# FFN grid values turned in bfloat16 apart from their scales, the first pass rebuilt, and a new order of work

## The chip, the core and the metric

The kernel runs on one core of a Trainium2 chip. A core has a matrix engine (TensorE, PE in the profile, with its weight loads shown as PEld), a vector engine (VectorE, DVE), a scalar engine (ScalarE, ACT), a general engine (GpSimd, POOL) and an engine that starts transfers (SyncE, SP; its queue is SPq). Each works through its own instructions in the order in which they were written into its queue, and waits on semaphores for the others. The metric is the device time of one execution in microseconds (us); the kernel before takes 1528.81 us, the median of three runs (1525.49 to 1529.01).

## What is computed

A small transformer stack on x of 4 x 2048 x 256 in float32:

```python
x = x + attn_a(layernorm(x))      # random-feature form; q and k divided by the norm of the whole tensor
x = x + ffn(layernorm(x))
x = x + attn_b(layernorm(x))      # 16 heads, attention over the first axis of 4
x = x + ffn(layernorm(x))

def fp4_quant_dequant(x):         # blocks of 16 along the last axis
    scale = max(max(abs(xb)) / 6, 1e-12)
    idx = searchsorted(MID, abs(xb / scale))
    return GRID[idx] * sign(xb) * scale     # GRID = 0, .5, 1, 1.5, 2, 3, 4, 6

def ffn(x):                       # 256 -> 704 -> 256
    gate = q(x) @ q(w_gate).T
    y = q(x) @ q(w_up).T
    return q(silu(gate) * y) @ q(w_down).T  # q is fp4_quant_dequant
```

In attn_a the quotient of the two feature maps needs, besides x, only the two norms of q and k over all tokens. They are found from the gram matrix of the normalized x, before any token can be projected.

## The kernel before

The 2048 positions are cut into 16 groups (`NJ`) of 128; a group holds the 4 tokens (`S`) of each of its positions, 128 partitions by 4 x 256. `first_pass` goes over all groups once: it loads x (tile `x`, L312), takes mean and variance on DVE (`bn_stats` L595, `bn_aggr` L596 into `moments`), the inverse root on POOL (`roots`, L363 and around), normalizes on ACT (L392) and adds up the gram in two PSUM banks on PE (L563). Beside this the weights are loaded, folded (L818), centred (L850) and, for the FFN, quantized and turned (L709 to L762). At its end the gram is weighed with the weights (L916 to L919), multiplied and summed on DVE (`sum_products`, L939 and L940), the norms' roots are taken on ACT, and the weights of the feature maps are joined by them (`join_weights`, L986 and L987). Only then can the first projection (L1076, `wvz`) start.

`group(j)` writes the work of one group: `attention_a`, an FFN, `attention_b`, a second FFN. An FFN has `ffn_in`, once for the group's four tokens, and `ffn_tile`, once for each token. Both call `quantize` (from L1108). For the hidden values (128 x 704) it runs:

- DVE: block maxima (L398) and their reciprocals (L399) into `sh`; ACT: maxima by 1/6 (L1123)
- DVE: values over scales (L403, into `qa`, float32)
- ACT: steps of the grid (L409, into `qm`, bfloat16)
- DVE: two passes (L416 `to_sum`, L419 `from_sum`) that leave the grid value, signed, in `qa`
- POOL: grid values by scales (L1151, in place in `qa`)
- PE: six transposes of 128 x 128 in float32 into two PSUM banks (L1349); ACT: two copies into `hqT` (L1361)
- PE: six matmuls of the down projection (L1372)

The input (128 x 1024, tiles `xn`, `qax`, `qmx`, `sx`) goes the same way and is turned by `turn` (L1053, L1060) into a tile of the pool `turned`, from which the gate and up projections read (L1294). A float32 matmul appears as two records in the trace, a transpose as one.

The order is made when the program is built. Each piece of work is an `op` with an engine, an estimated duration, a rank and what it reads and writes. `Plan.order` simulates the engines and takes, for each engine that is free, the ready op of lowest rank whose buffers are to be had; DVE and POOL ops with `port=True` are not laid beside each other. A group's ranks begin at the six numbers of its row in the table `BEGIN` (attention a, first FFN's input and tiles, attention b, second FFN's input and tiles). `order(24)` tries 24 orders, one by the ranks and 23 with ranks shaken by random numbers, and keeps the one that ends first in this simulation. The chosen order is the order of instructions on every engine. The pools have few tiles (two `qax`, one `qmx`, four `qa`, two `qm`, five `sh`, two `hqT`, eight PSUM banks), and an op that needs one waits until the last user of it has ended.

Of the kernel before, what the change touches and what calls it, by code (L numbers as in the profile page):

```python
# [57 lines left out]
class Plan:  # L58
# [55 lines left out]
    def order(self, tries):  # L114

        ends = [(self.order_of(i)[0], i) for i in range(tries)]
        return self.order_of(min(ends)[1])[1]

    def order_of(self, seed):
# [57 lines left out]
        while left:  # L177
# [56 lines left out]
            if not times:  # L234
                return math.inf, []
# [14 lines left out]
        return now, [i for _, i in out]  # L250
# [3 lines left out]
def kernel(  # L254
# [74 lines left out]

    moments = one([P, NJ, S, 2], "moments")  # L330
    half_moments = one([P, 6], "half_moments")
# [25 lines left out]
    def root_of(v, y, t, half):  # L357

        power(v, y, half)
        newton(v, y, t)  # L360

    def power(v, y, half):
        nc.gpsimd.tensor_tensor(y, v, half, ALU.pow)  # L363

    def newton(v, y, t):
        nc.gpsimd.tensor_mul(t, y, y)
        nc.gpsimd.tensor_mul(t, t, v)
        nc.gpsimd.tensor_scalar(t, t, -0.5, 1.5, ALU.mult, ALU.add)
        nc.gpsimd.tensor_mul(y, y, t)
# [48 lines left out]
    def from_sum(a, m):  # L418
        nc.vector.scalar_tensor_tensor(a, m, FLOOR, a, ALU.max, ALU.subtract)  # L419
# [16 lines left out]
    tiles("qax", 2, [P, S * D], fp)  # L436
    tiles("qmx", 1, [P, S * D], fp, BF16)
    tiles("sx", 3, [P, 3, S * D // BLK], fp)
    tiles("sil", 2, [P, HF], fp)
    tiles("qa", 4, [P, FF], fp)  # L440
    tiles("qm", 2, [P, FF], fp, BF16)
    tiles("sh", 5, [P, 3, FB], fp)
    tiles("hqT", 2, [P, 6, P], fp)
# [14 lines left out]
    def first_pass():  # L458
# [5 lines left out]
        for b in XN:  # L464
            nc.gpsimd.memset(b.ap[:, :, D : D + 1], 1.0)
        WQK, PROD, WNAT = (plan.given("pp", 0) for _ in range(3))
# [16 lines left out]
        sums, part, ssq, bsq, rn = (  # L483
            one([P, 2], t) for t in ("sums", "part", "ssq", "bsq", "rn")
        )
# [55 lines left out]
        def normalized_products(n, j):  # L541
# [15 lines left out]
            def products(n=n, xn=xn):  # L557
                for s in range(S):
# [11 lines left out]
            op(  # L570
                "PE",
                2.62,
                AHEAD + 3.0 * n + 9,
                products,
                [(xn, s) for s in range(S)],
                [(b, 0) for b in GRAM],
            )

        for n, j in enumerate(order):
            X = kept[j % len(xs_of)]  # L580
            xj = X.ap
            own = [(X, s) for s in range(S)]
            op(
                "SP",
                1.8,
                AHEAD + 3.0 * n - 40.0,
                lambda xj=xj, j=j: load_x(xj, j),
                (),
                own,
                land=3.0,  # L590
            )

            def stats(xj=xj, j=j):
                for s in range(S):
                    nc.vector.bn_stats(half_moments, xj[:, s, :])  # L595
                    nc.vector.bn_aggr(moments[:, j, s, :], half_moments)  # L596

            op("DVE", 2.35, AHEAD + 3.0 * n, stats, own, [("moments", j)])

            if n == 0 or n % 2:  # L600
                js = slice(j - 1 if n > 1 else j, j + 1)

                def roots(js=js):
                    mean, var = (moments[:, js, :, i] for i in range(2))
                    y, off, v, t = (norm_tiles["a"][:, js, i, :] for i in range(2, 6))
                    nc.gpsimd.tensor_scalar(v, var, 1.0, LN_EPS, ALU.mult, ALU.add)
                    root_of(v, y, t, nhalf[:, : js.stop - js.start, :])
                    nc.gpsimd.tensor_mul(off, mean, y)
                    nc.gpsimd.tensor_scalar(off, off, -1.0, 0.0, ALU.mult, ALU.add)

                js = range(js.start, js.stop)
                op(
                    "POOL",
                    3.3,
                    AHEAD + 3.0 * n + 3,
                    roots,
                    [("moments", i) for i in js],
                    [(("a", i), "rstd") for i in js],
                )
                for i in js:  # L620
                    normalized_products(order.index(i), i)
# [265 lines left out]
        def sum_biases():  # L887
            v = squares.ap[:, : 2 * D]
            nc.vector.tensor_mul(v, grow, grow)
            nc.vector.tensor_reduce(  # L890
                bsq, v.rearrange("p (t m) -> p t m", t=2), AX.X, ALU.add
            )

        op(
            "DVE", 1.4, AHEAD + 30.0, sum_biases, [(GROW, 0)], [(squares, 0), ("bsq", 0)], port=True
        )
        def take_g00():
            nc.vector.tensor_copy(g00, gram[0][:, :P])
# [5 lines left out]
        def take_sums():  # L904
            nc.vector.tensor_scalar_mul(sums[:, 0:1], gram[0][:, D : D + 1], 2.0)
            nc.vector.tensor_scalar_mul(sums[:, 1:2], gram[1][:, P : P + 1], 2.0)
# [4 lines left out]
        for c in range(KC):  # L911
            mm = plan.buf("mm")

            def weigh(c=c, mm=mm):
                if c == 0:
                    nc.tensor.matmul(mm.ap, g00, wqkA[:, 0, :], start=True, stop=True)  # L916
                else:
# [13 lines left out]
                    ALU.mult,  # L931
                    ALU.add,
                ),
                [(mm, 0), (GROW, 0), (G, 2)],
                [(PROD, c)],
            )

# [767 lines left out]
```

## Time and profile before

| | |
|---|---|
| median of three runs | 1528.81 us |
| the profiled execution's own time | 1528.71 us |
| its span, first to last instruction | 1526.9 us |
| mean granted clock of TensorE | 0.995 |

The page is one execution on the chip. Busy time is summed by engine and by groups of like instructions; a group's row has the line, the engine and the operation, what it writes and reads, partitions by elements, how often, busy time and mean duration, and then the engine's idle time just before them with what ended it. The two groups of this kernel's rows that fill the most time are the gate and up projections (L1294, 637.6 us) and the down projection (L1372, 350.1 us), both on PE; DVE has no such row, but five of about 120 to 130 us each, most of them passes of the quantization. Ends of matmuls are modelled and include the drain of the pipeline, so the time for which a matmul holds PE is read from start to start.

A row of stretches has the stretch, its length, then for PE, PEld, DVE, ACT and POOL the busy time and number of instructions, then the granted clock (1.00 is full), the busy share of the DMA engines and GB/s.

### The profile page before, as it was taken

The page shows a single profiled execution, that of the slowest core. Times are in us where ns is not written, and L with a number is a line of the kernel's source. Part 1 is how long each engine was busy: PE and PEld are TensorE (multiplying, and loading weights), DVE is VectorE, ACT ScalarE, POOL GpSimd, SP SyncE. Part 2 cuts the span into 40 slices and gives each one's busy share as a digit, 9 for nine tenths or more (in the row PEclk, how much of TensorE's full clock was granted, in tenths as well). Part 3 has the DMA queues.
Part 4 walks back from the last instruction along what each step waited for, and adds up shares of the span by engine and source line. Part 5 has one row for each costly group of instructions (what it writes and reads, how often), then busy time and mean ns, then how long its engine had stood idle before and what let it go on. Part 6 is the DMA issues. An engine that isn't in the chain of part 4 may idle for free.

```text
span 1526.9 us, 18822 instructions
## 1 busy us (share of the span) xinstructions
PE 1500.2 (98%) x6354; PEld 1074.1 (70%) x6354; DVE 1402.8 (92%) x2288; ACT 812.5 (53%) x1742; POOL 699.2 (46%) x738
## 2 busy tenths in 40 slices
PE   6989999999999999999999999999999999999999
PEld 5846766777676677777767776776766677777776
DVE  7988999999999999999998999989898999999995
ACT  5655655465463564464645445564646563554452
POOL 5333443346544552635446264453534435454531
PEclk9999999999999999999999999999999999999999
DMA  8300000000000000000000010000000000000000
GB/s 251 105 10 1 1 1 0 8 4 22 4 22 4 4 8 8 21 1 21 22 7 8 7 36 4 8 7 25 8 4 4 1 4 4 6 10 4 21 18 21
DMA packets 28976, 27.68 MB, mean 18 GB/s; under 512 B 3536, under 2 KB 28624, under 8 KB 28880
## 3 DMA queue, kind: packets, MB, share of 16 engines
q1 hardware_dynamic: 28880, 26.49, 5.5%
q8 instruction: 50, 0.82, 0.2%
q14 instruction: 46, 0.38, 0.1%
HBM read 18.09 MB, written 8.39 MB: 17 GB/s over the span
## 4 chain that ended last, share of the span: by engine, by line
PE 83%; DVE 12%; ACT 2%; issue 2%; DMA 1%; POOL 1%; SPq 0%; ACTq 0%; DVEq 0%; POOLq 0%
PE bank L1294 35%; PE bank L1076 20%; PE bank L1372 19%; PE bank L1349 5%; PE bank L1053 4%; DVE half_moments L595 1%; DVE qa L416 1%; DVE qa L403 1%; DVE h L1326 1%; DVE pp L1477 1%; DVE sh L398 1%; DVE qa L419 1%; DVE sc L1484 0%; DVE moments L596 0%; DVE pp L1603 0%
## 5 line engine op out<-in xcount | busy, mean ns | idle before, releaser
L1294 PE MATMUL bank<-wguT,turned 128*128 128x352 f32 x2048 | 637.6, 459 | 0.6 <-DVE h L1326 0.6
L1294 PEld LDWEIGHTS bank<-wguT,turned 128*128 128x128 f32 x2048 | 381.4, 190 | 193.8 <-issue 11.3
L1151 POOL TENSOR_TENSOR qa<-qa,sh 128x704 f32<-128x704 f32 x128 | 211.9, 1656 | 408.8 <-DVE qa L419 333.7
L1372 PE MATMUL bank<-wdT,hqT 128*128 128x256 f32 x1536 | 350.1, 379 | 0.0
L1372 PEld LDWEIGHTS bank<-wdT,hqT 128*128 128x128 f32 x1536 | 289.5, 190 | 51.9 <-issue 4.3
L1315 ACT ACTIVATE sil<-bank 128x352 f32<-128x352 f32 x256 | 117.0, 459 | 127.5 <-PE bank L1294 113.2
L409 ACT ACTIVATE qm<-qa 128x704 bf16<-128x704 f32 (+2 forms) x136 | 106.2, 783 | 104.1 <-DVE qa L403 102.0
L1361 ACT COPY hqT<-bank 128x256 f32<-128x256 f32 (+1 forms) x256 | 110.9, 481 | 85.2 <-PE bank L1349 84.4
L1326 DVE TENSOR_TENSOR h<-sil,bank 128x352 f32<-128x352 f32 x256 | 128.6, 510 | 27.1 <-PE bank L1294 16.8
L1585 POOL TENSOR_TENSOR pp<-vg,sc 128x1024 f32<-128x1024 f32 x64 | 132.4, 2088 | 19.1 <-DVE tok L1606 17.8
L416 DVE SCALAR_TENSOR_TENSOR qa<-qm,qa 128x704 f32<-128x704 bf16 (+2 forms) x136 | 130.6, 961 | 7.8 <-ACT qm L409 7.2
L403 DVE SCALAR_TENSOR_TENSOR qa<-sh,h 128x704 f32<-128x704 f32 x128 | 128.6, 1008 | 2.0
L419 DVE SCALAR_TENSOR_TENSOR qa<-qm,qa 128x704 f32<-128x704 bf16 (+2 forms) x136 | 124.1, 914 | 2.1
L1076 PE MATMUL bank<-wvz,turned 128*128 128x512 f32 x256 | 121.0, 608 | 3.6 <-DVE wvz L987 2.4
L398 DVE TENSOR_REDUCE sh<-h 128x44 f32<-128x748 f32 x128 | 119.0, 930 | 3.6
L1060 ACT COPY turned<-bank 128x512 f32<-128x512 f32 x160 | 87.0, 592 | 63.4 <-PE bank L1053 58.0
L1076 PE MATMUL bank<-wqkB,turned 128*128 128x512 f32 x256 | 120.4, 593 | 0.0
L1151 POOL TENSOR_TENSOR qax<-qax,sx 128x1024 f32<-128x1024 f32 x32 | 68.2, 2133 | 101.9 <-DVE qax L419 96.6
L1349 PEld LDWEIGHTS bank<-ident,qa 128*128 128x128 f32 x768 | 90.7, 141 | 29.3 <-issue 13.1
L1349 PE MATMUL bank<-ident,qa 128*128 128x128 f32 x768 | 105.7, 273 | 0.5 <-ACT turned L1060 0.3
L348 ACT ACTIVATE dev<-x,norms_f 128x256 f32<-128x256 f32 x128 | 65.0, 508 | 44.5 <-DVE x L342 41.5
L1076 PEld LDWEIGHTS bank<-wvz,turned 128*128 128x128 f32 x256 | 48.0, 195 | 50.6 <-issue 39.9
(168 smaller groups left out, 2119.6 us busy)
## 6 DMA issues: line engine op xcount, KB each, us to landing
x<-in_L_attn_a_x_dram SPq DMA_DIRECT2D x24, 512.0 KB, 4.3
out_dram<-x SPq DMA_DIRECT2D x64, 128.0 KB, 1.7
hqT<-in_L_ffn_w_down_dram SPq DMA_DIRECT2D x2, 352.0 KB, 2.8
hqT<-in_L_ffn_w_gate_dram SPq DMA_DIRECT2D x5, 128.0 KB, 4.5
hqT<-in_L_ffn_w_up_dram SPq DMA_DIRECT2D x5, 128.0 KB, 2.1
pp<-in_L_attn_a_Wq_dram SPq DMA_DIRECT2D x2, 256.0 KB, 4.2
pp<-in_L_attn_a_Wk_dram SPq DMA_DIRECT2D x2, 256.0 KB, 5.1
wvz<-in_L_attn_a_Wv_dram SPq DMA_DIRECT2D x1, 256.0 KB, 5.1
```

Source lines behind the costliest of these rows:

```text
L398: nc.vector.tensor_reduce(amax, src, AX.X, ALU.max, apply_absolute_value=True)
L403: nc.vector.scalar_tensor_tensor(blocks(a), over_blocks(rs), -6.0 * BELOW, src, ALU.mult, ALU.mult)
L416: nc.vector.scalar_tensor_tensor(a, m, FLOOR, a, ALU.max, ALU.add)
L419: nc.vector.scalar_tensor_tensor(a, m, FLOOR, a, ALU.max, ALU.subtract)
L1076: nc.tensor.matmul(bank.ap[:, :n], lhs.ap[:, c, s * P : (s + 1) * P], w[:, c, :], start=(c == 0), stop=(c == KC - 1),)
L1151: lambda: nc.gpsimd.tensor_mul(blocks(a.ap), blocks(a.ap), over_blocks(q.ap[:, 1, :])),
L1294: nc.tensor.matmul(bank.ap[:, :HF], xqT.ap[:, c, s * P : (s + 1) * P], w[:, c, cols], start=(c == 0), stop=(c == KC - 1),)
L1315: lambda g=g, sil=sil: nc.scalar.activation(sil.ap, g.ap[:, :HF], AF.Silu),
L1326: lambda u=u, sil=sil, half=half: nc.vector.tensor_mul(h.ap[:, half * FB // 2 : (half + 1) * FB // 2, :BLK], blocks(sil.ap), blocks(u.ap[: ...
L1349: nc.tensor.transpose(bank.ap[:, (i - i0) * P : (i - i0 + 1) * P], qa.ap[:, HC[i] : HC[i] + P], ident,)
L1372: nc.tensor.matmul(o.ap[:, :D], hqT.ap[:, i, :], wdT[:, i, :], start=(i == 0), stop=(i == 5),)
L1585: nc.gpsimd.tensor_mul(pv.ap.rearrange("p t (n e) -> p t n e", e=HD), vg.ap[:, :, :D].rearrange("p t (n e) -> p t n e", e=HD), over_blocks ...
```

## The change

Four things.

**The FFN's values are turned without their scales.** `from_sum` now writes the grid values, which are exact in bfloat16, into the bfloat16 tile. The scale product before the transposes goes, and with it the ACT product by 1/6. The grid values are turned by bfloat16 transposes (into one bank read as bfloat16), and ACT copies them back to the bfloat16 tile (`qm`, `qmx`). The maxima are turned by themselves (`scales_turned`: one float32 transpose, a copy by 1/6 on ACT into `sT`), and SP spreads each turned row over the 16 partitions of its block by DMA, straight into `hqT` or `turned`: eight rows of 128 numbers, each written 16 times, 64 KB in one transfer; six transfers for a hidden tile, eight for an input. POOL then multiplies the copied values into the spread scales, in place, and PE's projection reads the product.

**The first pass.** The first load of x comes in four pieces. `bn_aggr` goes: `bn_stats` writes its two halves' means and variances for all groups into an unused part of a tile, and mean and variance are put together for a group at once, for the first three groups on DVE with the root on ACT, for the later ones in pairs on POOL. The gram's products are an op for each token instead of one for all four. The bias terms of the norms are summed ahead (`times_biases`), and each half of the weighed gram is multiplied and summed in one instruction with `accum_out`; five small matmuls add up the parts. The weights are joined in two halves.

**The pools** are cut differently.

**The order.** `order(0)` takes the one order by the ranks, and `BEGIN` has other numbers; the first group's ranks now lie among those of the first pass (which run from -350 up).

```diff
-    order = plan.order(24)
+    order = plan.order(0)
...
-    tiles("qax", 2, [P, S * D], fp)
-    tiles("qmx", 1, [P, S * D], fp, BF16)
-    tiles("sx", 3, [P, 3, S * D // BLK], fp)
+    tiles("qax", 1, [P, S * D], fp)
+    tiles("qmx", 2, [P, S * D], fp, BF16)
+    tiles("sT", 2, [S * D // BLK, P], fp)
+    tiles("sx", 2, [P, 3, S * D // BLK], fp)
...
-    tiles("qa", 4, [P, FF], fp)
-    tiles("qm", 2, [P, FF], fp, BF16)
-    tiles("sh", 5, [P, 3, FB], fp)
-    tiles("hqT", 2, [P, 6, P], fp)
+    tiles("qa", 3, [P, FF], fp)
+    tiles("qm", 4, [P, 6 * P], fp, BF16)
+    tiles("sh", 4, [P, 3, FB], fp)
+    tiles("hqT", 3, [P, 6, P], fp)
...
-        (160, 226, 202, 285, 260, 357),
-        (242, 270, 276, 370, 420, 434),
...
+        (-192, -130, -62, -192, 24, 94),
+        (30, 12, 85, 183, 69, 266),
...
-            op(
-                "POOL",
-                us["scale"],
-                at + 6,
-                lambda: nc.gpsimd.tensor_mul(
-                    blocks(a.ap), blocks(a.ap), over_blocks(q.ap[:, 1, :])
-                ),
...
+                "DVE",
+                us["pass"],
+                at + 4.1,
+                lambda: from_sum(a.ap, *2 * (m.ap[:, : n],)),
                 [(a, 0)],
+                [(m, 0)],
                 port=True,
+            )
...
+        def scales_turned(at, q, n, dst, pieces):
+            bank, sT = plan.buf("bank"), plan.buf("sT")
...
+                lambda: nc.tensor.transpose(bank.ap[:n, :P], q.ap[:, 0, :], ident),
...
+                lambda: nc.scalar.mul(sT.ap[:n], bank.ap[:n, :P], 1.0 / 6.0),
...
+            def spread():
+                for to, g in pieces:
+                    nc.sync.dma_start(
+                        to(),
+                        sT.ap[g : g + P // BLK].unsqueeze(1).to_broadcast([P // BLK, BLK, P]),
+                    )
+            op(
+                "SP",
+                0.45 * len(pieces),
+                at + 1,
+                spread,
+                [(sT, 0)],
+                [(dst, "scale")],
+                land=2.0,
+            )
...
+            def turn_hidden():
+                for i, f in enumerate(HC):
+                    nc.tensor.transpose(
+                        bank.ap.bitcast(BF16)[:, i * P : (i + 1) * P],
+                        qm.ap[:, f : f + P],
+                        ident16,
+                    )
...
+                lambda: nc.scalar.copy(
+                    qm.ap, bank.ap.bitcast(BF16)[:, : 6 * P]
+                ),
...
+                lambda: nc.gpsimd.tensor_mul(
+                    hqT.ap, hqT.ap, qm.ap.rearrange("p (c n) -> p c n", n=P)
+                ),
+                [(qm, 0), (hqT, "scale")],
+                [(hqT, 0)],
+                port=True,
```

And of the first pass:

```diff
-            def stats(xj=xj, j=j):
                 for s in range(S):
-                    nc.vector.bn_stats(half_moments, xj[:, s, :])
-                    nc.vector.bn_aggr(moments[:, j, s, :], half_moments)
...
+                for s0, s1 in [(s, s + 1) for s in range(S)] if n == 0 else [(0, S)]:
...
+                        lambda xj=xj, j=j, s=s: nc.vector.bn_stats(
+                            moments[:, j, s, :], xj[:, s, :]
+                        ),
...
+            if n >= SOON:
+                op("POOL", 4.4, at + 3.0, lambda cut=cut: roots_later(cut), seen, done)
+            else:
...
+                op("DVE", 0.8, at + 0.5, lambda cut=cut: variances(cut), seen, done)
...
+                    lambda y=y, v=v: nc.scalar.activation(y, v, AF.Sqrt),
...
+                op("DVE", 1.0, at - 30.0, lambda cut=cut: inverses(cut), (), done)
...
-            nc.vector.tensor_mul(prod, prod, wqkA)
-            nc.vector.tensor_reduce(
-                part, prod.rearrange("p c (t m) -> p t c m", t=2), AX.XY, ALU.add
-            )
...
+                    nc.vector.scalar_tensor_tensor(
+                        prod[:, c, cols],
+                        mm.ap[:, cols],
+                        1.0,
+                        wqkA[:, c, cols],
+                        ALU.mult,
+                        ALU.mult,
+                        accum_out=part[:, 3 + c, t : t + 1],
+                    )
```

## The prediction

> **What bounds the kernel now.** I read the page's busy shares first, then its chain.
>
> ```profile
> PE 1500.2 (98%) x6354; PEld 1074.1 (70%) x6354; DVE 1402.8 (92%) x2288; ACT 812.5 (53%) x1742; POOL 699.2 (46%) x738
> ...
> PE 83%; DVE 12%; ACT 2%; issue 2%; DMA 1%; POOL 1%; SPq 0%; ACTq 0%; DVEq 0%; POOLq 0%
> ```
>
> TensorE (PE) is nearly always busy and carries 83% of the chain, but VectorE (DVE) at 92% is close behind. An average hides stages, so next the busy time by stretch (columns: PE, PEld, DVE, ACT, POOL, clock, DMA share, GB/s).
>
> ```profile
> 0.00:20.00 20.00, 6.89 (x32) 6.00 (x32) 14.00 (x47) 5.87 (x10) 9.14 (x40) 1.00 0.89 274
> 60.00:80.00 20.00, 16.31 (x95) 12.74 (x94) 19.51 (x42) 10.55 (x22) 5.17 (x4) 0.98 0.15 46
> 100.00:150.00 50.00, 46.88 (x160) 28.43 (x159) 44.48 (x73) 27.27 (x60) 19.34 (x29) 0.93 0.00 1
> 700.00:900.00 200.00, 199.94 (x854) 144.13 (x854) 186.51 (x281) 102.12 (x221) 96.25 (x84) 1.00 0.04 12
> 1300.00:1400.00 100.00, 100.00 (x413) 70.23 (x412) 96.12 (x147) 50.28 (x104) 47.21 (x44) 1.00 0.02 7
> 1500.00:1527.00 27.00, 23.63 (x119) 19.54 (x116) 13.38 (x21) 7.39 (x17) 4.16 (x3) 0.99 0.09 30
> ```
>
> From 200 to 1400 us PE is busy 1197.9 of 1200 us: a us taken off PE there can be a us off the end, as long as DVE (1119.7 of 1200, 93.3%) keeps up. The idle 26.8 us of the span lie at the edges: 13.1 in the first 20 us, 3.7 in 60 to 80, 3.1 in 100 to 150, 3.4 at the end. PE's waits by releaser name them.
>
> ```profile
> PE bank L563 <- ACT vg L392: 11.4, 1, 11.4
> PE bank L1076 <- DVE wvz L987: 2.4, 1, 2.4
> PE bank L563 <- ACT vz L392: 1.9, 1, 1.9
> ```
>
> The first is the way from the first load of x to the first product, the second the joined weights after the first pass, the third a late norm.
>
> **FFN transposes on PE.** The groups, and one of the stretches in order of time:
>
> ```profile
> L1349 PE MATMUL bank<-ident,qa 128*128 128x128 f32 x768 | 105.7, 273 | 0.5 <-ACT turned L1060 0.3
> L1053 PE MATMUL bank<-ident,qax 128*128 128x128 f32 x256 | 35.0, 278 | 0.8 <-ACT turned L1060 0.8
> ...
> 808.44 0.82 PE L1349 MATMUL bank<-ident,qa 128*128 128x128 f32 x6
> 809.10 2.53 PE L1294 MATMUL bank<-wguT,turned 128*128 128x352 f32 x8
> ```
>
> The 0.82 us holds the pipeline's drain; what PE is really held for is start to start, 809.10 - 808.44 = 0.66 us for six, 0.109 us each. Removed: (768 + 256) x 0.109 = 111.8 us. Added: 160 transposes of the scales (32 + 128), still float32 with 128 moving columns, so 0.109 each: 17.5 us. And 1024 bfloat16 transposes, of which the trace has none. Bounds: in the chain 16 records of L1294 (352 columns) take 4.73 us, 0.296 each, and 8 of L1076 (512 columns) 3.44, 0.430 each, so PE is paid by the column, 0.84 ns in float32, and 128 columns are the 0.109. Half the bytes at half the time is the lower end, 0.0545; no faster at all, 0.109, the upper. The Trainium skill speaks against the low end: "TensorE: Matmul & The Clock Gate", section "Back-to-back issue gap", has about 81 ns as the pace of a stream of weight-load and matmul pairs with 128 columns, against 56 ns for a matmul alone. Each of these transposes is such a pair (in the changed order a weight load of its own stands before each). By the row the net is 111.8 - 55.8 - 17.5 = -38.5 us, by the rule 111.8 - 82.9 - 17.5 = -11.4; at 0.109 it is +17.3. In the float32 rows the weight load is hidden (PEld overlaps, only 13.1 us of "issue" before 768 of them), and a load of half the bytes should hide likewise, so I take 0.060, near the row: 61.4, **net -32.9 us**. The added wait: PE now meets the block maxima early, at the scales' transpose, and all its work stands behind that; I cost it with the leads below.
>
> **DVE.** Passes are as many as before; the last writes bfloat16 but reads the same float32, so its 0.93 us (L419, 704 columns) stays: no reason for loss or gain beyond some hundredths. The aggregates of the first pass go (L596, 64 x 0.182 = 11.7 us); 27 small operations of about 0.17 us for three early norms come (+4.6); the bias and weight sums trade about evenly. DVE then needs about 1395 us. PE's 1500 us shrink by 2.2%, so DVE's share from 200 to 1400 us becomes 93.3% / 0.978 = 95.4%. The stretch 1300 to 1400 above ran 96.1% with PE at 100%, so DVE can go there.
>
> **GpSimd (POOL).** The scale products go (211.9 + 68.2 = 280.1 us); products of 768 columns (128 x 1.656 x 768/704 = 231) and of 512 (64 x 1.07, half of 2.133 = 68) come: 299, +19 us on an engine at 46%. Second operands in bfloat16 are not in the trace; half or 1.3 times the time would leave POOL at 55% at most. POOL's products hold DVE up in either version: the DVE pass at 802.30 takes 1.63 us instead of 0.89 beside a POOL product of 1.93. 19 us more of it at that ratio cost DVE at most 8 us, 0.5% of share.
>
> **ACT.** 160 scale products (30.7 + 8.2) go, 160 small copies of about as much come; two copies into hqT (0.58 + 0.38) become one of 768 columns, about 0.85 by L409 (0.79 for 704). ACT stays near 53%.
>
> **The spread.** New is a path beside the data: scales turned on PE, copied on ACT, six (hidden) or eight (input) DMAs on SP, 1024 in all of 64 KB, then POOL. Before, SP only had loads and stores; behind a spread that waits for its copy now stand later spreads, the stores and the reloads of x, none of which is short of time. One issue takes 0.33 to 0.5 us of SP in the trace, so some 410 us of SP in all. Behind POOL's product, which now waits for the landing, stand the next tile's product and the norm roots, and ACT's normalizing behind those.
>
> ```profile
> out_dram<-x SPq DMA_DIRECT2D x64, 128.0 KB, 1.7
> ...
> q1 hardware_dynamic: 28880, 26.49, 5.5%
> ```
>
> A store of 128 packets lands after 1.7 us, so six land 5 x 0.4 + 1.7 = 3.7 us after the first issue. The skill speaks against this too ("DMA: Bandwidth & Descriptors", "Why a DMA increments its semaphore by 16 and not by 1"): a transfer runs on the largest number of engines up to 16 that divides the slowest dimension of both sides. Here that is 8 source rows and 128 target rows: 8 engines, 16 packets each. At 46.5 ns a packet (5.5% of 16 x 1526.9 us by 28880) that is 0.74 us each and, if all six share the same eight, 4.5 + 1.7 = 6.2 us. What is needed from the end of a scales' transpose to the down projection is 0.3 (copy) + spread + 0.1 + 1.5 (product): 5.6 or 8.1 us. In the changed order of PE I added up the work that stands between the two, for each of 128 tiles: least 7.5 us, ten under 8.1, median 18; for the 32 inputs least 6.0, then 8.9. So the row costs nothing here, the rule 2.8 + 2.7 us. From the last data transpose to its projection the lead is 5.2 us in the median, and 2.4 to 2.6 us of ACT and POOL are needed; three tiles of 128 fall short, by under 3 us each. I take **+6 us** for these, for the higher DVE share and for POOL; 0 and 15 are the ends. A third hqT and four qm pay for the longer hold; one qax and three qa instead of two and four, the other ranks and the single order I cost at nothing by themselves: PE's median lead from a tile's last transpose to its projection was 2.35 us before, by the same count, and cost no idle time.
>
> **First part.** The first load comes in four pieces. The last of them, issued by 0.72 + 3 x 0.5 and taking 3 (between 1.7, the store, and 4.25, the whole first load), lands at 5.2; last statistics 0.43, four small DVE operations 0.7, root on ACT 0.3, five more 0.9, normalize 0.6: first product near 8.5 instead of 11.44 us, -2.9. After the gram, the weights were joined 12.4 us later (66.7 to 79.1) with 3.7 idle; product and sum over both halves (1.23 + 1.22) and two of L926 go, four of about 0.45 come. The fill has also moved earlier (transposes of three blocks of x now stand inside the pass), so I count only -2. **-5 us**, between 0 and -9.
>
> **Sum**, against the profiled execution (1528.7 us, span 1526.9; the median shown is 1528.8): 1528.7 - 32.9 - 5 + 6 = **1497 us**.
>
> **Rivals.**
> - Forecast: PE stays the bound, 1497; its own range 1482 to 1510. 64%.
> - DVE becomes the bound. For it: 95.4%, and a port shared with a busier POOL. Against: 96.1% was seen. If DVE cannot pass 94%, the 1200 us shrink to 1119.7 / 0.94 = 1191, some 10 us over all: 1528.7 - 5 - 10 = 1513. 18%.
> - The spread comes late, the slower side. For it: loads took 4 to 6 us to land when DMA was 80% busy, and 131072 packets now come. Against: at 46.5 ns these are a quarter of 16 engines. Adding up what the shortest leads lack, the whole gain is gone when a spread takes 8.0 us from first issue to last landing; at 9.1 the loss is 50.7 + 9.9 us: 1557. 12%.
> - The bfloat16 pairs keep 81 ns: 1528.7 - 11.4 - 5 + 6 = 1518; without any speedup 1547. 6%.
>
> About 0.3% (4.6 us) can be told from no change. Faster takes the forecast, most of the second and two thirds of the last: 0.84; same 0.05; slower 0.11. The range 1478 to 1522 goes from half the row, the full -9 and no stall (1481, some 3 us less if the stage around 100 us fills) up to the 81 ns with a poorer first part.
>
> **What would show it.** Right: the bfloat16 transposes six in about 0.36 us start to start, PE 97% or more with DVE near 95%, first product before 9.5 us. Wrong: POOL's product in the FFN waiting for a DMA by tens of us in total, PE's projection L1534 waiting for POOL, or PE below 96% between 200 and 1400 us.

## The result, and the profile after

| | before | after |
|---|---|---|
| median | 1527.15 us (1525.0 to 1529.01, 4 runs) | 1674.16 us (1672.4 to 1679.73, 4 runs) |
| span of the profiled execution | 1526.9 us | 1670.6 us |
| TensorE idle in it (span less busy) | 26.7 us | 149.4 us |
| mean granted clock of TensorE | 0.995 | 0.973 |

The changed kernel takes 1.0969 times as long, 95% interval 1.0945 to 1.0992: slower by 147 us, where 31 us less was forecast. The rival on the slower side, the late spread, had the right mechanism but 1557 us.

The page of the changed kernel, the parts that answer to those shown of before (busy time, DMA, the chain, and the two groups around the spread):

```profile
PE 1521.2 (91%) x6522; PEld 1046.9 (63%) x6522; DVE 1424.3 (85%) x2266; ACT 802.1 (48%) x1617; POOL 733.2 (44%) x782
...
DMA packets 168310, 95.02 MB, mean 57 GB/s; under 512 B 11776, under 2 KB 167936, under 8 KB 168192
...
q1 hardware_dynamic: 168192, 93.63, 29.7%
...
PE 61%; DVE 15%; DMA 9%; POOL 6%; issue 3%; ACT 3%; SPq 2%; POOLq 0%; ACTq 0%; DVEq 0%
...
L1523 POOL TENSOR_TENSOR hqT<-hqT,qm 128x768 f32<-128x768 f32 x128 | 229.7, 1798 | 523.6 <-DMA hqT<-sT 271.5
L1534 PE MATMUL bank<-wdT,hqT 128*128 128x256 f32 x1536 | 376.4, 399 | 76.0 <-POOL hqT L1523 74.5
```

PE is at 91% and DVE fell from 92 to 85%. The chain holds DMA (9%), GpSimd (6%) and SP's queue (2%), which had 1, 1 and 0 before. So transfers, and engines that wait for them, now stand in the way. The waits name them (from where, total us, times, longest; the whole execution):

```profile
POOL hqT L1523 <- DMA hqT<-sT: 271.5, 44, 18.7
...
PEld bank L1534 <- POOL hqT L1523: 94.2, 50, 6.5
...
ACT sT L1236 <- DMA hqT<-sT: 75.5, 27, 8.2
```

GpSimd's product waits for the spread, and the down projection waits for the product. The third line is a wait that the prediction did not have: ACT needs one of the two `sT` tiles for the next turned scales, and the spread is not through with them. Here is one such place in the chain (start, us, what), and beside it SP's timeline:

```profile
831.15 0.97 PE bank L1153 x4
832.12 0.34 PE bank L1502 x6
832.46 0.65 PE bank L1441 x3
833.11 3.87 DMA hqT<-sT
...
837.14 2.23 POOL hqT L1523
839.37 0.04 issue
839.42 2.86 PE bank L1534 x12
```

```profile
815.79 5.18 SPq L1243 DMA_DIRECT2D hqT<-sT  x6
821.07 6.62 SPq L1574 DMA_DIRECT2D out_dram<-x  x2
829.12 4.65 SPq L1243 DMA_DIRECT2D hqT<-sT  x6
```

The six transfers of this tile are issued from 829.12 and the last has landed at 836.98, 7.9 us later; the product then takes 2.23, and PE gets its operand at 839.4. The stretches show that it is so all the way (columns as before: PE, PEld, DVE, ACT and POOL busy, clock, DMA share, GB/s; the first row is the kernel before, the other two the change):

```profile
200.00:1400.00 1200.00, 1197.93 (x5028) 853.67 (x5029) 1119.65 (x1760) 641.03 (x1380) 568.64 (x546) 1.00 0.03 9
...
200.00:1400.00 1200.00, 1102.18 (x4670) 749.90 (x4669) 1043.04 (x1600) 584.27 (x1167) 541.73 (x521) 0.97 0.29 52
...
1300.00:1400.00 100.00, 89.58 (x405) 63.40 (x404) 81.06 (x122) 41.38 (x84) 45.46 (x36) 0.98 0.31 52
```

PE was busy 1197.9 of these 1200 us before, and is now 1102.2, at a clock of 0.97 instead of 1.00. With the clock's share taken as (1 - mean clock) x span, the 143.7 us by which the span grew split into: idle +122.7; clock +37.5 (45.1 against 7.6); PE's work at full clock, busy less the clock's share, -16.5 (1476.1 against 1492.6). This split is an estimate from the mean clock.

### The profile page after: what moved, and what is told of

Its sections match the earlier page's. It is cut to its first block, busy times and chain, and to the rows that moved or that the text cites. A ratio compares the mean times of both kernels' runs of the same rounds, so it can differ in the third digit from the quotient of the medians.

```text
span 1670.6 us, 21837 instructions
## 1 busy us (share of the span) xinstructions
PE 1521.2 (91%) x6522; PEld 1046.9 (63%) x6522; DVE 1424.3 (85%) x2266; ACT 802.1 (48%) x1617; POOL 733.2 (44%) x782
## 2 busy tenths in 40 slices
DMA packets 168310, 95.02 MB, mean 57 GB/s; under 512 B 11776, under 2 KB 167936, under 8 KB 168192
## 4 chain that ended last, share of the span: by engine, by line
PE 61%; DVE 15%; DMA 9%; POOL 6%; issue 3%; ACT 3%; SPq 2%; POOLq 0%; ACTq 0%; DVEq 0%
PE bank L1441 24%; PE bank L1534 16%; PE bank L1153 14%; DMA hqT<-sT 8%; POOL hqT L1523 4%; PE bank L559 2%; SPq L1243 2%; PE bank L1502 2%; PE bank L1130 2%; DVE qm L401 1%; DVE sh L380 1%; DVE qa L398 1%; DVE h L1473 1%; DVE pp L1639 1%; DVE qa L385 1%
## 5 line engine op out<-in xcount | busy, mean ns | idle before, releaser
L1523 POOL TENSOR_TENSOR hqT<-hqT,qm 128x768 f32<-128x768 f32 x128 | 229.7, 1798 | 523.6 <-DMA hqT<-sT 271.5
L1534 PE MATMUL bank<-wdT,hqT 128*128 128x256 f32 x1536 | 376.4, 399 | 76.0 <-POOL hqT L1523 74.5
L1534 PEld LDWEIGHTS bank<-wdT,hqT 128*128 128x128 f32 x1536 | 300.0, 199 | 146.7 <-POOL hqT L1523 94.2
L1236 ACT ACTIVATE sT<-bank 44x128 f32<-44x128 f32 (+1 forms) x160 | 42.3, 267 | 217.8 <-PE bank L1228 110.5
L398 DVE SCALAR_TENSOR_TENSOR qa<-qm,qa 128x704 f32<-128x704 bf16 (+2 forms) x136 | 129.8, 956 | 17.5 <-ACT qm L391 17.3
L1513 ACT COPY qm<-bank 128x768 bf16<-128x768 bf16 x128 | 100.8, 794 | 77.2 <-PE bank L1502 74.6
L401 DVE SCALAR_TENSOR_TENSOR qm<-qm,qa 128x704 bf16<-128x704 bf16 x128 | 133.9, 1049 | 3.5
L1422 POOL TENSOR_TENSOR turned<-turned,qmx 128x512 f32<-128x512 f32 x64 | 83.7, 1322 | 117.7 <-ACT qmx L1412 73.7
L335 DVE SCALAR_TENSOR_TENSOR x<-bank,x 128x256 f32<-128x256 f32 x128 | 51.9, 414 | 38.9 <-PE bank L1534 30.0
L1153 PE MATMUL bank<-wvgB,turned 128*128 128x288 f32 x256 | 75.3, 418 | 7.7 <-ACT sT L1236 7.7
L1639 DVE TENSOR_TENSOR pp<-qk 128x1024 f32<-128x1024 f32 x64 | 81.5, 1274 | 0.2
```

Source lines behind the costliest of these rows:

```text
L401: nc.vector.scalar_tensor_tensor(a if to is None else to, m, FLOOR, a, ALU.max, ALU.subtract)
L1153: nc.tensor.matmul(bank.ap[:, :n], lhs.ap[:, c, s * P : (s + 1) * P], w[:, c, :], start=(c == 0), stop=(c == KC - 1),)
L1523: lambda: nc.gpsimd.tensor_mul(hqT.ap, hqT.ap, qm.ap.rearrange("p (c n) -> p c n", n=P)),
L1534: nc.tensor.matmul(o.ap[:, :D], hqT.ap[:, i, :], wdT[:, i, :], start=(i == 0), stop=(i == 5),)
```

## The experiments

Times are medians; each ratio is to the kernel before, run on the same chip. "Forecast" in the texts on record means the prediction's 1497 us. The changed kernel's spread is issued at L1243; the lines of the groups shift by a few from kernel to kernel. The order of work is made anew for each kernel, from its operations and their prices. In the traces the matrix, vector and scalar engines run their work in the same order in the change, e1, e2, e7, e10 and e15; in e5 and e17 they share another order, in e6 and e9 a third, in e11 and e14 a fourth. A difference within one of these sets is the edit's; across sets, the order is in it too.

### What the spread costs: without it, with fewer rows, from two queues, with true prices

**e1_none** leaves the spread out and fills the tiles with ones at the start, so the scales are missing from the output:

```diff
+    for t in plan.pools["turned"] + plan.pools["hqT"]:
+        nc.vector.memset(t, 1.0)
...
-                for to, g in pieces:
-                    nc.sync.dma_start(
...
+                pass
```

> The changed kernel with its order kept, but the spread's transfers left out (its computation is left out: POOL multiplies into ones or old values). Theory S (the spread is late: SP needs 4.7 to 5.2 us to issue six transfers and they land about 8 us after the first issue): the waits for it go, and 1490 to 1515 us are left, near the forecast. Rival O (the new order, ranks and pools lack slack by themselves): 1600 us or more. In between, both share.

1549.28 us, ratio 1.0137 (1.0067 to 1.0208). The nine fills hold up the first pass: its first projection starts 7.3 us later than in the change, so some 1542 without them (an estimate; the two runs were 1544.91 and 1553.66). The spread costs about 132 us, give or take 5; a loss of some 14 against before is left, and the forecast is missed even without the spread.

**e2_rows** issues as many transfers, each with 8 rows instead of 8 x 16 (15 of 16 rows keep the ones of the fill):

```diff
+                    nc.sync.dma_start(to()[: P // BLK], sT.ap[g : g + P // BLK])
```

> As many transfers as in the change, each of 8 rows instead of 128 (the spreading over 16 partitions is left out). Theory S-issue (the price is SP's, by the instruction): issues still take 0.6 to 0.7 us, the time stays above 1600 us. Theory S-packets (the price is by the packet, in the issue or on the 8 engines): issues fall to 0.5 us or less, landing comes at once, and the time falls to 1500 to 1540 us.

1553.46 us, ratio 1.0165 (1.0132 to 1.0197), four us over e1, which is no more than e1's own two runs differ. An issue takes 0.62 us of SP in the median here, not much less than in the change (0.71), as the first theory had it, but the time is near the second's. So 1024 issues on SP are nearly free; the packets that they carry are not.

**e3_two** issues every second transfer from ACT's queue:

```diff
+                for i, (to, g) in enumerate(pieces):
+                    (nc.scalar if i % 2 else nc.sync).dma_start(
```

> Every second transfer of a spread is issued from ACT's queue instead of SP's, same order. S-issue: SP's stretch for six halves to about 2.5 us, POOL's wait for the spread falls by a third or more, 1580 to 1640 us. S-packets: the 8 engines carry the same packets, no gain, 1660 us or more; ACT, held by its issues of 0.7 us each, may add to it.

1808.3 us, ratio 1.1832 (1.1789 to 1.1876). The second queue does not help, and ACT, which has work to do, now stands while it issues (durations ns least/median/most):

```profile
L1243 ACTq DMA_DIRECT2D hqT<-sT x384: 611/1176/2625, 136.8 to 1790.6; - x192
```

SP's own half took 618 ns in the median.

**e4_plan** tells the planner what a transfer costs:

```diff
-                0.45 * len(pieces),
+                0.86 * len(pieces),
...
-                land=2.0,
+                land=3.3,
```

> The planner alone is told the spread's measured price: 0.86 us of SP for each transfer instead of 0.45, landing 3.3 us later instead of 2.0. Theory S: the order puts work between and wins back a part, 1540 to 1640 us, with less waiting of PE for POOL's product (74.5 us in the change). Rival O: the time stays within 1% of 1674.

1630.13 us, ratio 1.0666 (1.0635 to 1.0698). GpSimd's wait for the hidden tiles' spread fell from 271.5 to 155.2 us. So another order, made for dearer transfers, wins back 44 of the 147 us. Whether it is the truer prices that do this, or only that the order is another, this run does not part.

### Eight engines or sixteen

**e5_dup** keeps 128 packets in each transfer but gives it 16 source rows. ACT writes each scale twice, side by side, before the scales are turned, so each turned row stands twice and is written 8 times from each:

```diff
+            op("ACT", 0.26, at - 4,
+                lambda: nc.scalar.mul(
+                    blocks(twice(), 2), over_blocks(q.ap[:, 0, :], 2), 1.0 / 6.0),
+                [(q, 0)], [(q, 1)])
...
+                    r = 2 * P // BLK
+                    nc.sync.dma_start(
+                        to(), sT.ap[2 * g : 2 * g + r].unsqueeze(1).to_broadcast([r, P // r, P]))
```

> Each scale is written twice side by side by ACT before it is turned, so that a transfer has 16 source rows, each written 8 times, instead of 8 written 16 times; 128 packets as before, and 0.26 us more of ACT for each quantization. Theory E8 (the transfer is split over as many engines as divide the rows of both sides, 8 of the 16, and these are the bound): issue falls to about 0.6 us or less, a spread lands 2 to 3 us earlier, 1570 to 1620 us. Rival P (the packets cost the same whatever the split, or the reading from few partitions does): within 1% of 1674 us.

1577.66 us, ratio 1.0336 (1.0315 to 1.0356): 96 us less with the same packets of data. But the operation added on ACT also gave this kernel another order, so the 96 are not the engines' alone. The cleaner pair is this run and e17 below, which has the same order and doubling and no spread: 1556.41 us, so that the spread over sixteen engines costs 21 us (with what the moments' own tile, in e17 alone, brings), where over eight it cost some 132 in the change's order.

That the engines are eight and sixteen can be seen in the DMA share (the last column but one, a share of 16 engines) while a spread is under way, first in the change, then in e5_dup:

```profile
831.00:835.00 4.00, 4.00 (x20) 2.76 (x19) 3.65 (x6) 1.51 (x3) 0.00 (x0) 1.00 0.44 79
...
828.00:831.50 3.50, 3.50 (x14) 2.23 (x13) 2.32 (x5) 0.46 (x1) 2.22 (x2) 1.00 0.75 98
```

In the mean 0.44 x 16 = 7.0 engines are busy in the first, which fits eight, and 0.75 x 16 = 12.0 in the second, which is more than eight. The small packets in the page's DMA line count them:

```profile
DMA packets 176502, 95.05 MB, mean 60 GB/s; under 512 B 19968, under 2 KB 176128, under 8 KB 176384
```

Without a spread (e10, below) 3584 packets are under 512 B, in the change 11776, here 19968. The 1024 transfers of the spread add 8192 and 16384, 8 and 16 each. The Trainium skill ("DMA: Bandwidth & Descriptors", "Why a DMA increments its semaphore by 16 and not by 1") says that each engine taking part ends with one write to the semaphore; the count agrees with eight and sixteen engines. A hidden tile's six transfers, with the packets of the trace counted off in order, were landed 7.7 us after the first issue in the median of the change's 128 tiles (7.2 to 9.2), and 5.4 in e5 (5.2 to 6.6). GpSimd's wait for the hidden tiles' spread is 104.5 us here, against 271.5.

### The first pass by itself

**e6_first** is the kernel before with the new first pass alone (the loads in pieces, the moments and roots by groups, the products by token, the join in halves).

> The kernel before with the new first pass alone (FFN, pools, table of ranks and 24 tries as before). As forecast: 5 us less than before, 1519 to 1527. By the trace of the change, where the first projection started at 80.6 instead of 79.1 us: no gain, 1527 to 1532.

1544.81 us, ratio 1.0123 (1.0106 to 1.014), above both forecasts. The first product came at 8.66 us as forecast, but the first projection at 87.51, where before had it at 79.08. Its waits from 0 to 80 us:

```profile
ACT qk L378 <- POOL norms_a L619: 15.2, 4, 6.5
...
PE bank L558 <- ACT qk L378: 10.0, 3, 4.8
...
POOL qk L611 <- PE bank L558: 7.3, 2, 4.2
```

The last line is odd: GpSimd's roots wait for the products, which come after them. They share a tile: the moments stand in spare columns of `qk`, and `qk` also takes every fourth normalized sub-tile. The planner's tokens keep the two apart, but the program's waits are made by tile. So it was tried to part them.

**e9_first_own**:

```diff
-        MOMENTS = XN[3]
+        MOMENTS = plan.given("qax", 0)
```

> The kernel before with the new first pass alone, as e6_first (1544.81 us), but the moments of the tokens lie in a tile of their own (the buffer of the first FFN quotients, which the first pass does not use) and no longer in spare columns of the tile that also takes every fourth normalized sub-tile. Theory false waits (writes of moments, normalized values and the products' reads of the shared tile wait for one another, which the planner's finer tokens do not know): most of e6's 17 us goes, 1524 to 1533 us, and POOL's waits for the products and the scalar engine's for the roots (15.2 us) shrink below 5. Rival (the new order of the first pass itself, its roots on GpSimd or its loads): unchanged, 1540 to 1548.

1528.49 us, ratio 1.0007 (0.9998 to 1.0016): all of the 16 us is gone with this line, in the same order of work, and with it the waits above; the first projection starts at 73.08. The tile that was shared cost the 16 us. The 6 us by which this pass is now earlier than the old one bring nothing at the end.

### What the bfloat16 turning brings by itself

**e7_none_dve** has no spread either; GpSimd multiplies by a tile of ones, and `to_sum` of the hidden values is left out (so scales and that pass are missing from the output), some 122 us of DVE.

> Spread left out (POOL multiplies by ones), and of the hidden values one of DVE's passes, the first of the two after ACT, left out too (the other squares the values instead): 128 x 0.95 = 122 us of DVE less, same order. e1 without its fills is 1542. Theory D (the rest of e1 over the forecast is DVE, 94.5% busy there, being late at PE): 1500 us or less. Rival R (ranks, first pass and tail): 1530 or more.

1527.53 us, ratio 0.9998 (0.9991 to 1.0006). **e8_none_free** is the same with `to_sum` kept, and with the spread that is not there priced at next to nothing in the planner, so that the order need not leave room for it:

```diff
-                0.45 * len(pieces),
+                0.02 * len(pieces),
...
-                land=2.0,
+                land=0.1,
```

> Spread left out (POOL multiplies by ones) and priced at nothing by the planner, ranks as in the change, so the order is made for what runs. Theory D: the order can do little, 1530 to 1545. Rival R: the planner's wrong prices made the order, 1500 to 1520.

1559.33 us, ratio 1.0216 (1.0195 to 1.0236), 10 over e1, and 17 over e1 less its fills, instead of less: an order that is tighter by the planner's book was worse on the chip. Neither of these two runs fell where one of its texts had it. **e10_none_own** takes the ones and the spread's old prices, with the moments apart.

> The change without its spread DMAs (GpSimd multiplies by a tile of ones, so the output is without the scales), moments in their own tile. It leaves the bf16 turning, the turned scales and the multiply. Theory that the first pass costs 17 us by false waits and that DVE at 94% of the stretch takes most of the 33 us that TensorE is spared: 1549 less the 7 us of the fills less 12 to 17, 1521 to 1530. Rival (first pass costs by its own work): 1538 to 1545. If DVE did not bind, 1500 or less.

1538.87 us, ratio 1.007 (1.0052 to 1.0088): in the rival's range, though e9 had cleared the first pass of the cost that the rival names. Its page, and the stretch from 200 to 1400 us:

```profile
PE 1484.1 (97%) x6522; PEld 1031.9 (67%) x6522; DVE 1425.2 (93%) x2267; ACT 801.3 (52%) x1617; POOL 740.2 (48%) x782
...
DMA packets 29025, 27.70 MB, mean 18 GB/s; under 512 B 3584, under 2 KB 28672, under 8 KB 28928
...
PE 63%; DVE 29%; issue 4%; ACT 3%; POOL 1%; DMA 1%; SPq 0%; DVEq 0%; ACTq 0%; POOLq 0%
```

```profile
200.00:1400.00 1200.00, 1169.77 (x5098) 808.79 (x5097) 1134.08 (x1735) 628.69 (x1260) 595.61 (x568) 0.99 0.03 9
```

DVE is busy 94.5% of this stretch, and PE has 30 us of gaps where it had 2. PE's work at full clock is 1470.3 us (1484.1 - 0.009 x 1535.7), 22 less than before and 28 less than in e9 (1501.4 - 0.002 x 1526.5 = 1498.3), whose FFN is still the old one: the saving is there. It came back as idle time (51.6 us against 26.7) and clock. DVE carries 29% of the chain, against 12% before. In e7, where DVE has 114 us less to do (1311.3) and the moments are not yet apart, it carries 9%, and the time is 11 us lower. So DVE takes a part of the saving, not all. Two single gaps make 12 of the 30 us, 6.3 at 322 us and 5.7 at 1178; both stand in e7 too (5.5 and 5.7), in the same order, so the lighter DVE did not close them.

### What is left at sixteen engines

**e11_dup_own** is e5 with the moments apart and the planner told 0.6 us and 3.0; **e12_dup_begin** the same with the old `BEGIN`.

> The change with 16 source rows to a transfer as e5_dup (1577.66 us), moments in their own tile, and the planner told measured prices of a transfer (0.6 us on SP, 3.0 to land, against 0.45 and 2.0). Theory: first pass gives 12 to 17, the prices up to 15 (the waits of GpSimd's product for the spread fall): 1545 to 1562. If the spread's packets themselves cost the rest (contention with loads of x and stores), no better than 1565.

> As e11_dup_own, but with the table of stages' begins of the kernel before. Theory that the order matters by no more than some 10 us either way once DVE is the bound: 1540 to 1572. If the new table is itself the loss: below 1535; if the old table starts spreads too late: above 1580.

1583.22 us (1.0369, 1.0343 to 1.0395) and 1575.39 us (1.0313, 1.0298 to 1.0329): neither is a gain on e5 beyond what orders differ among themselves, and neither met its theory. In e11 SP stood 207 us waiting for the last residual add before it could issue a store, and GpSimd 138 us for the spread; so stores at the head of SP's queue were suspected.

```diff
-                    at + 23,
+                    at + 35,
                     lambda: nc.sync.dma_start(out[s, j * P : (j + 1) * P, :], xs(s)),
```

**e13_late_store** (on e11), **e15_after_late** (on the change) and **e16_late_begin** (on e12):

> e11_dup_own (1583.22 us) with the 64 stores of finished rows ranked 12 us later, so that they stand further behind on SP's queue. Theory head-of-line (on SP's one in-order queue a store that waits for the last residual add, 207 us of waits in e11, holds the spreads behind it, and GpSimd's products with them): SP's wait for the add falls below 70 us, GpSimd's wait for the spread (138 us) at least halves, 1550 to 1565 us. Rival (the stores are issued late because everything else is; they hold nobody): 1578 to 1588.

> The change as it is (1674.16 us) with the 64 stores ranked 12 us later and nothing else. Theory head-of-line by stores: of 109 us in which SP waited for the last residual add most is gone and 20 to 50 us come off, 1625 to 1655. Rival (8 engines carry the packets too slowly and the stores don't matter): 1668 to 1680.

> e12_dup_begin (1575.39 us) with the later stores: by the head-of-line theory 1545 to 1560, by its rival 1570 to 1580.

1592.15 us (1.0427, 1.0408 to 1.0446), 1672.53 us (1.0956, 1.093 to 1.0981) and 1583.07 us (1.0365, 1.035 to 1.038). Nothing is won, but the rank did not do its part either: SP still waits 223 us for the add in e13 and 106 in e15. The traces settle what these runs could not. Setting the end of each of ACT's copies into `sT` beside the first issue of its spread, matched in order, one finds that in all of the change SP stood at a store's own wait with a spread ready behind it for 2.3 us, in e11 for 1.9 of its 207. The stores hold hardly anybody. **e14_one_piece** does more:

```diff
-                for to, g in pieces:
+                for to, g in pieces[:1]:
...
-                    hqT.ap, hqT.ap, qm.ap.rearrange("p (c n) -> p c n", n=P)
+                    hqT.ap, ones.unsqueeze(1).to_broadcast([P, 6, P]), qm.ap.rearrange("p (c n) -> p c n", n=P)
```

> e11_dup_own with only the first of each spread's six or eight transfers; GpSimd multiplies by ones (the scales are left out of the output) but still waits for that one transfer, which writes into the tile of the product. Planner's prices and order are e11's. Theory that the issue time of six in a row on SP (3.8 us a tile) is what is left of the loss: 1540 to 1552, near e10_none_own (1538.87). Rival (the wait in order itself, a store ahead of it or a buffer not yet free, whatever follows): 1565 to 1583.

1576.52 us, ratio 1.0322 (1.0304 to 1.0339), 7 less than e11. Its waits:

```profile
ACT sh L1234 <- DVE sh L380: 121.5, 80, 7.2
...
POOL hqT L1539 <- DMA hqT<-sT: 13.2, 3, 7.1
```

GpSimd hardly waits for a spread any more, and the time is nearly the same. L1234 is the doubling that e5 brought in. ACT reaches it before DVE has the scales and stands there, with its other copies behind; this was suspected next.

**e17_double_alone** adds this doubling to e10; **e18_dup_at** moves it 4 us later in e5 and parts the moments.

> e10_none_own (no spread, GpSimd multiplies by ones, so the scales are left out of the output; 1538.87 us) with the doubling of the scales on the scalar engine added (160 operations, 35 us busy in e14), planner's prices 0.45 and 2.0 as in the change. Theory that the repair's own operation costs what e14 could not get back (in e14 the scalar engine stood 121 us before it, waiting for DVE, with the other evictions behind): 1555 to 1572. Rival (the loss of e14 is the planner's larger prices, which put the tiles further apart): 1537 to 1546.

> e5_dup (1577.66 us) with the moments in their own tile and the doubling ranked 4 us later, beside the scales' transpose. Theory of the doubling's place: the scalar engine's waits for DVE's scales fall and 10 to 20 us come off, 1555 to 1568. Rival (prices or the spread itself): 1570 to 1582.

1556.41 us (1.0185, 1.0168 to 1.0202) and 1572.71 us (1.0291, 1.0276 to 1.0307). The kernel with the doubling takes 17.5 us more than e10. This is the operation and the other order that comes with it; no run parts the two. Moving the doubling (e18) gained 5 us on e5, and parting the moments may have a share in them. e14, with one transfer of six and larger prices in the planner, is 20 us above e17; those prices were no gain here. No version was found that beats the kernel before.

## Why the prediction was wrong, step by step

- **bfloat16 transposes: right.** The timeline of the changed kernel:

```profile
817.72 0.50 PE L1502 MATMUL bank<-ident,qm 128*128 128x128 bf16 x6
...
818.06 0.81 PE L1441 MATMUL bank<-wguT,turned 128*128 128x352 f32 x2
```

  Six take 818.06 - 817.72 = 0.34 us start to start, 0.057 each, where the row gave 0.0545, 0.060 was taken, and the Trainium skill's "Back-to-back issue gap" ("TensorE: Matmul & The Clock Gate") had 0.081. The row decided rightly, for the six in a row that stand here. PE's work fell by 22 to 28 us in e10, for a net 32.9.
- **The spread: the failed step.** The prediction had the right rule before it (eight rows, eight engines) and kept the row of a store instead, whose transfer has 128 source rows: 3.7 us for six, at no cost. In the change they took 7.7 us in the median, and the eight transfers of an input 9.0, and leaving the spread out took some 132 us off the time (e1). The price by the rule, 6.2 us (4.5 for the packets and 1.7 to land), was too small as well: the sixth issue was over after 4.8 us in the median, and the last landing came 2.9 us after it. The break-even that the prediction named, 8.0 us, was thus all but reached by one spread alone.
- **The spread priced alone, not in its queue.** Leads were compared with one spread on an empty SP. In the trace of the change a spread was first issued 2.1 us in the mean (at most 23.5) after its scales lay ready in `sT`, 334 us over the 160 tiles. In 196 of these SP was issuing earlier spreads, in 22 loads and stores. The rest were waits of the spread itself or of one before it. SP's own waits point to the tile that a spread is written into, which an earlier down projection still read; for this longer hold the prediction had counted on the third `hqT`:

```profile
SPq L1243 <- PE bank L1534: 175.9, 158, 20.3
```

  Two `sT` tiles then hold ACT (75.5 us), which no step named. The longest wait of a product was 18.7 us. This is the likely reason why 132 us came, and not the rival's 29 over before; no run takes the queue away and leaves the landing.
- **SP's queue "none of which is short of time"**: the number of issues was indeed nearly free (e2), though they held SP for 781 us and not for 410, and stores held the spreads by 2.3 us only. But the spreads themselves were short of time, and held each other.
- **DVE "can go there": failed, in two terms.** One stretch of before at 96.1% was read as a pace that can be kept; without the spread DVE stood at 94.5% from 200 to 1400 us, PE had gaps, and e10 is 10 us slower than before. And DVE's work did not fall to the 1395 us of the forecast. With the new first pass and the old FFN (e9) it was 1389.1 us, with the new FFN as well (e10) 1425.2: 36 us more, where 8 were allowed for GpSimd's products beside it. The last pass, before and in e10:

```profile
L419 DVE SCALAR_TENSOR_TENSOR qa<-qm,qa 128x704 f32<-128x704 bf16 x130 | 120.4, 927 | 2.1
...
L401 DVE SCALAR_TENSOR_TENSOR qm<-qm,qa 128x704 bf16<-128x704 bf16 x128 | 131.7, 1032 | 3.5
```

  It is not the bfloat16 result that costs: passes with no GpSimd operation beside them took 0.884 and 0.885 us in the mean. Those beside one took 1.05 us before (34 of 130) and 1.34 in e10 (41 of 130). The rival with DVE as the bound named a part of the cause, at too low a price (1513); e7 shows that it is not the whole.
- **Ranks and the single order at nothing: not separated, and doubtful.** e4, e8 and e12 changed only prices or begins and moved the time by -44 us, by +10 (17 if the fills of e1 are taken off) and by -8. Even e7, without spread and with DVE relieved, is 30 us over 1497. What of this is the order, and what the first pass, stays open; that orders differ by tens of us is shown, so the term should not have stood at nothing.
- **First part, -5: failed.** The first product came at 7.64 us (8.5 forecast), so the way to it was right. The shared tile then cost 16 us when the pass was alone (e6 against e9). In the change without spread, parting the tile let the first projection start 9.8 us earlier (71.9 us in e10, 81.8 in e7 of the same order), but the end came only some 3 us earlier (1542, an estimate, to 1538.87); what took up the rest was not looked into.
- **GpSimd and ACT durations: right.** The product of 768 columns took 1.798 us (1.806 forecast); that of 512 took 1.322 (1.07), 16 us in all on an engine at 44%. What they do to DVE stands above.
- **What the prediction named as signs of being wrong** came just so: GpSimd waiting for a DMA, L1534 waiting for GpSimd, PE below 96% between 200 and 1400 us.

## What to carry to other kernels

A row of a trace prices a new instruction only if it has the shape that sets its time. The row of the float32 transposes had the same 128 columns and was right; the row of the store had 128 source rows, the spread has 8, and it was wrong by a factor of two. A DMA between tiles on the chip is to be priced by how many engines its source rows give it, by what stands before it in its queue, and by when the tile that it writes into comes free. When the bound engine is at 98% and the next at 93%, relief of the first may be worth only what the second can still follow; a single busy stretch does not show what it can keep up, and its own work can grow through what runs beside it. A run that adds an operation also gets another order here: compare it with a run of that same order. Spare columns of a tile in use are not a free place: what the tile's other user does came back as waits, though the planner counts them apart.

## What the runs showed of the hardware that was not expected

- Long gaps on TensorE cost more than themselves. In the trace's record of its granted clock it is one half in single stretches of 3.4 us or a multiple of that, and full otherwise. The change has 21 of them, 91.5 us in all, of which half is lost, and all but the last, at the end, come just after a gap of 2.1 us or more. Before had 4, 16.2 us in all. One of the change, after a gap of 5.7 us:

```profile
1280.70:1287.50 6.80, 5.59 (x13) 4.52 (x14) 4.69 (x6) 2.56 (x5) 4.61 (x7) 0.50 0.32 49
```

  Idle time alone does not set it: e17, with 68 us of idle time but no gap over 3 us, has 18.0 us at half clock and a mean of 0.995; e10, with 52 us but gaps of 5.7 and 6.3, has 27.7 and 0.991. No length of gap parts the two cases cleanly: in the kernel before one of 1.7 us was followed by such a stretch, in the change some over 2 us were not.
- The issue of a transfer from tile to tile held SP longer than loads and stores did, and its least time went with the shape of the source: 607 ns with 8 rows in the change, 544 with 16 in e5_dup, though both write 128 rows. The medians, 711 and 549, agree with an SP that is held longer when eight engines carry the packets: with a sixteenth of the packets in each transfer (e2) the median is the least, 625 and 624.

```profile
L1243 SPq DMA_DIRECT2D hqT<-sT x768: 607/711/1845, 132.0 to 1657.1; - x192
```

```profile
L1258 SPq DMA_DIRECT2D hqT<-sT x768: 544/549/1630, 131.6 to 1563.6; - x192
```
